# Row maxima of two head groups in five units of score matmuls in place of six

## The chip, the cores and the metric

The kernel runs on one core of a Trainium2 chip. The metric is the device time of one execution in microseconds (us), as the median of several runs. The engines are TensorE (PE in the profile; PEld is its weight load), VectorE (DVE), ScalarE (ACT), GpSimd (POOL) and SyncE (SP, which issues most DMAs). TensorE writes into PSUM, and the other engines read it from there.

## The reference

One decoder layer for B = 4 batches of S = 512 positions and D = 512 features, 16 heads of 32 features, all in fp32. Each of the three parts adds to `x`:

```python
x = x + self_attention(layernorm(x))      # q, k, v and output projections with biases, causal
x = x + cross_attention(layernorm(x), ctx)  # q = layernorm(x), k = v = ctx, causal with a bias of -10000
h = layernorm(x)
shared = relu(h @ W_up.T) @ W_down.T
rw = softmax(top_2(h @ W_gate.T))         # 8 experts
x = x + shared + sum(rw) * (h @ W_expert)
```

Self attention: `softmax(where(causal, q k^T / sqrt(32), -inf)) v`. Cross attention fills masked scores with -10000 in place of -inf.

## The kernel before

All weights stay in SBUF. A head group `g` is four heads: 4 x 32 = 128 features, one chunk of 128 partitions, so there are four groups. The 512 positions make four blocks of 128.

**Two passes over the scores.** The softmax needs each row's maximum before the exponentials. `with_maxima` computes scores with queries on the partitions (tile `sm`) only to get the maxima; `attend` computes them again with keys on the partitions (tile `sc`), subtracts the maximum by a matmul with a bf16 row (`mrow`), and takes the exponential.

**`maxima(g, blocks)`** (L267) does one unit. It takes two PSUM tiles of two banks each (`pair`; two heads per tile, one per bank), and for each block `i` and each head one matmul with 32 contracted rows: 128 queries of block `i` against the (i + 1) x 128 keys up to its end. Causality makes the width 128, 256, 384 or 512. Then for each of the two tiles ScalarE copies it to an SBUF tile `s` (L292), and GpSimd masks the diagonal squares (L298). The reductions on VectorE (L310, result `nm`) come back as a list of jobs. After block 3 of a group `split(g)` (L323) puts the maxima into bf16 parts in `parts[g % 2]`; `rows(g)` (L334) transposes these on TensorE (tile `mt`) and copies the result to `mrow` (L344).

**`with_maxima(steps, a, first, norms)`** (L780) goes through the units of the four groups: blocks (0, 1), block 2 and block 3 of each, twelve in all, with 384, 384 and 512 columns. Between the units it puts matmuls of other work (the fill) in portions by `cost`: query, key and value projections of this or the next batch, or the FFN of the batch before. While a unit's fill runs, the jobs of the unit before are handed to VectorE, one per fill matmul. `rows(g - 1)` goes into the fill of unit (g, 3), so three of the four transposes stand in the fill; the function returns group 3, which `attend` does at n = 4. `norms` are the layernorm jobs of the next batch, added to every other unit. In fill steps named `share` and `gate` a whole step counts as one; all others count as four matmuls.

**`attend(a, late)`** (L810) runs the units (0), (1), (2, 3) of key blocks of each group: scores and exponentials (L360 to L404), and two units later the product with the values (`values`, tile `pv`).

**What sets the order.** TensorE, VectorE, ScalarE and GpSimd take their instructions in the order in which the program writes them (`manual_schedule` with `BY_HAND`); only SyncE's DMAs are ordered by the framework. Semaphores are placed by the framework: a tile that reuses a buffer waits for the readers of the tile before it. PSUM has four pairs (`ps`, bufs=4), which `sm`, `sc`, `pv`, `mt` and the fill's accumulators share. The SBUF tiles `s` use the tags `pt0`, `pt1`, `pt2` (two buffers each) that the exponentials of `attend` use as well.

**The eight stages.** Each batch has one `with_maxima` for self attention and one for cross attention. Their fill has 36, 34, 34 and 16 steps (self, batches 0 to 3) and 20, 36, 20 and 25 steps (cross). Before a cross stage `norm_cross(e, made, t)` transposes the normalised rows in two halves, and ScalarE copies each half into `cqT` (L257), which holds the queries of that stage; one fill step (four matmuls) stands between the two calls for the halves, none after the second. In batch 0's self stage the first `skip` = 3 steps run before the units. The FFN's `gate` (L717) takes the top experts: four maxima and a chain of small operations on VectorE with one exponential on ScalarE within it.

Of the kernel before, what the change touches and what calls it, by code (L numbers as in the profile page):

```python
# [9 lines left out]
F32 = mybir.dt.float32  # L10
# [8 lines left out]
P = 128  # L19
# [7 lines left out]
def decoder_layer(  # L27
# [111 lines left out]
    for r in range(HG):  # L139
# [14 lines left out]
        pattern=[[-1, S]],  # L154
# [13 lines left out]
        pattern=[[-P, NT], [0, HG]],  # L168
# [91 lines left out]
    class Attention:  # L260
# [3 lines left out]
            self.more, self.sums, self.rden, self.e = {}, {}, {}, None  # L264
            self.added = () if cross else range(NC - 1)

        def maxima(self, g, blocks):  # L267

            if blocks[0] == 0:
                self.nm[g] = small.tile([P, NT, HG], F32, tag="nm", name=f"nm_{self.name}_{g}")
            first = blocks[0]
            scs = [pair(f"sm_{self.name}_{g}_{first}_{n}") for n in range(2)]
            at = {i: sum((k + 1) * P for k in blocks if k < i) for i in blocks}
            N = sum((i + 1) * P for i in blocks)
            for i in blocks:
                for r in range(HG):
                    h = slice(r * HD, (r + 1) * HD)
                    nc.tensor.matmul(  # L280
                        scs[r // 2][:, r % 2, at[i] : at[i] + (i + 1) * P],
                        lhsT=self.q_t[h, g, i * P : (i + 1) * P],
                        rhs=self.k_t[h, g, : (i + 1) * P],
                        start=(i == first),
                        stop=True,
                        skip_group_check=(i != first),
                    )
            made = []
            for n in range(2):
                W, tag = {0: (S, "pt0"), 2: (N, "pt1"), 3: (S, "pt2")}[first]  # L290
                s = work.tile([P, 2, W], F32, tag=tag, name=f"s_{self.name}_{g}_{first}_{n}")
                nc.scalar.copy(s[:, :, :N], scs[n][:, :, :N])  # L292
                if len(blocks) > 1:

                    diagonal = s.rearrange("p u (k q) -> p (u k) q", k=2)[:, :, :P]
                else:
                    diagonal = s[:, :, N - P : N]
                nc.gpsimd.affine_select(  # L298
                    out=diagonal,
                    in_=diagonal,  # L300
                    compare_op=ALU.is_ge,
                    fill=NEG,
                    base=0,
                    pattern=[[0, 2 * len(blocks)], [-1, P]],
                    channel_multiplier=1,
                )
                made.append(s)

            def largest(n, i):
                nc.vector.tensor_reduce(  # L310
                    self.nm[g][:, i, 2 * n : 2 * n + 2],
                    made[n][:, :, at[i] : at[i] + (i + 1) * P],
                    axis=AX.X,
                    op=ALU.max,
                    negate=True,
                )

            jobs = [(lambda n=n, i=i: largest(n, i)) for n in range(2) for i in blocks]
            if blocks[-1] == NT - 1:
                jobs.append(lambda: self.split(g))  # L320
            return jobs

        def split(self, g):  # L323
# [445 lines left out]
    def run(steps):  # L769
        for step in steps:  # L770
            for _ in step() or ():
                pass
# [7 lines left out]
    def with_maxima(steps, a, first=0, norms=()):  # L780


        norms = list(norms)
        run(steps[:first])
        fill = matmuls(steps[first:])
        total = sum(1 if step.__name__ in ("share", "gate") else NC for step in steps[first:])
        units = [(g, i) for g in range(NC) for i in ((0, 1), (2,), (3,))]
        cost = [sum(k + 1.5 for k in i) for _, i in units]
        done, due, jobs = 0, 0.0, []
        for n, (g, i) in enumerate(units):  # L790
            new = a.maxima(g, i)
# [12 lines left out]
            jobs = new  # L804
        for _ in fill:
            pass
        run(jobs)
        return NC - 1

    def attend(a, late):  # L810

        units = [(g, j) for g in range(NC) for j in ((0,), (1,), (2, 3))]
        waiting = []

        def values():
            g, j, pts = waiting.pop(0)
            a.values(g, j, pts)
            if g in a.added and j != (2, 3):
                a.add_up(*waiting[0])

        for n, (g, j) in enumerate(units):
            waiting.append((g, j, a.scores(g, j)))
            if n == 4:
                for copy in a.rows(late):
                    copy(nc.scalar.copy)
            if len(waiting) > 2:
                values()
            if a.cross and j == (0,):
                behind(a.e, g)
            if a.cross and j == (2, 3):  # L830
                a.masked(g)
        while waiting:
            values()

    with tc.manual_schedule(engines=BY_HAND):
        e, norms, turns = norm_in(0, x0)
# [3 lines left out]
        nc.gpsimd.tensor_scalar(bqs_sb, bq_sb, SCALE, None, ALU.mult)  # L840
        add_bias(e)
        between_self = query_key(e) + value(e)
        skip, between_cross, ahead = 3, [], []
        for b in range(B):
            more = b + 1 < B
            sa = Attention(e.q_t, e.k_t, e.v, False, f"s{b}")
            norms, turns = [], []
            if more:
                after, norms, turns = norm_in(b + 1)
            late = with_maxima(between_self, sa, skip, norms)  # L850
# [5 lines left out]
            made = out_projection(e, sa, context(e) + turns)  # L856
# [7 lines left out]
            late = with_maxima(steps[3:], ca)  # L864
# [7 lines left out]
            made = add_cross(e, ca)  # L872
# [20 lines left out]
            skip = 0  # L893
# [50 lines left out]
```

## Time and profile before

| | |
|---|---|
| median of three runs | 825.18 us (825.09 to 825.27) |
| the profiled execution | 825.04 us, span 823.3 us |
| busy: PE, DVE, ACT, POOL | 813.3, 544.6, 398.0, 298.3 us |
| reductions L310 | 256, 193.0 us |
| copies L292 of `sm`: 768 wide, 1024 wide | 128 of 0.80 us, 64 of 1.02 us |
| masks L298 | 192, 93.1 us |

The span is the time from the first to the last instruction. Busy time of an engine is the union of its instructions. Matmuls overlap each other in the trace, since the next one starts to stream before the last has drained; the distance between starts is what a matmul costs. A wait that is named after "<-" tells which engine's instruction ended the idle time. The timeline's lines give the start, the length, the engine, the line of the code, the operation, the tiles written and read, and the count.

### The profile page before, as it was taken

The page shows a single profiled execution, that of the slowest core. Times are in us where ns is not written, and L with a number is a line of the kernel's source. Part 1 is how long each engine was busy: PE and PEld are TensorE (multiplying, and loading weights), DVE is VectorE, ACT ScalarE, POOL GpSimd, SP SyncE. Part 2 cuts the span into 40 slices and gives each one's busy share as a digit, 9 for nine tenths or more (in the row PEclk, how much of TensorE's full clock was granted, in tenths as well). Part 3 has the DMA queues.
Part 4 walks back from the last instruction along what each step waited for, and adds up shares of the span by engine and source line. Part 5 has one row for each costly group of instructions (what it writes and reads, how often), then busy time and mean ns, then how long its engine had stood idle before and what let it go on. Part 6 is the DMA issues. An engine that isn't in the chain of part 4 may idle for free.

```text
span 823.3 us, 14456 instructions
## 1 busy us (share of the span) xinstructions
PE 813.3 (99%) x5800; PEld 368.8 (45%) x5800; DVE 544.6 (66%) x937; ACT 398.0 (48%) x502; POOL 298.3 (36%) x549
## 2 busy tenths in 40 slices
PE   8999999999999999999999999999999999999998
PEld 7344454444444454334534445444543444444543
DVE  2578735967678834587868873596779835887512
ACT  2456526762456515556155652676257814565110
POOL 4434512343334732224233471244234643343100
PEclk9999999999999999999999999999999999999999
DMA  9600000001010000030100000000102000000101
GB/s 340 236 27 15 1 1 1 2 2 52 1 39 14 2 1 1 0 103 2 52 14 14 1 2 0 1 2 2 53 3 74 29 1 0 1 2 2 52 0 51
DMA packets 13539, 24.54 MB, mean 30 GB/s; under 512 B 1952, under 2 KB 1952, under 8 KB 13472
## 3 DMA queue, kind: packets, MB, share of 16 engines
q1 hardware_dynamic: 13184, 23.09, 8.3%
q8 instruction: 45, 0.74, 0.4%
q10 hardware_dynamic: 288, 0.52, 0.2%
q14 instruction: 22, 0.18, 0.1%
HBM read 19.42 MB, written 4.19 MB: 29 GB/s over the span
## 4 chain that ended last, share of the span: by engine, by line
PE 94%; DVE 3%; ACT 1%; issue 1%; DMA 0%; POOL 0%; ACTq 0%
PE pm_qk L233 13%; PE pv_c L429 9%; PE pm_d L221 7%; PE pm_u L233 7%; PE pm_v L221 7%; PE pm_o L638 7%; PE pm_e L221 6%; PE pv_s L429 6%; PE sm_c L280 6%; PE sc_s L370 6%; PE sc_c L370 5%; PE sm_s L280 5%; DVE nm_s L310 1%; PE sc_s L381 1%; PE sc_c L381 1%; PE tp_x L666 1%
## 5 line engine op out<-in xcount | busy, mean ns | idle before, releaser
L310 DVE TENSOR_REDUCE nm_c<-s_c 128x2 f32<-128x256 f32 (+3 forms) x128 | 96.3, 810 | 36.6 <-POOL s_c L298 36.6
L310 DVE TENSOR_REDUCE nm_s<-s_s 128x2 f32<-128x256 f32 (+3 forms) x128 | 96.7, 810 | 24.4 <-POOL s_s L298 24.4
L292 ACT COPY s_s<-sm_s 128x768 f32<-128x768 f32 (+1 forms) x96 | 78.8, 874 | 69.0 <-PE sm_s L280 51.2
L292 ACT COPY s_c<-sm_c 128x768 f32<-128x768 f32 (+1 forms) x96 | 78.9, 875 | 48.7 <-PE sm_c L280 34.1
L402 ACT ACTIVATE pt_c<-sc_c 128x768 f32<-128x768 f32 (+1 forms) x96 | 78.5, 884 | 29.3 <-PE sc_c L381 24.8
L298 POOL TENSOR_SCALAR_AFFINE_SELECT s_c<-s_c 128x256 f32<-128x256 f32 (+1 forms) x96 | 46.5, 485 | 118.5 <-ACT s_c L292 117.4
L404 POOL TENSOR_SCALAR_AFFINE_SELECT pt_c<-pt_c 128x256 f32<-128x256 f32 (+1 forms) x96 | 57.4, 605 | 70.5 <-ACT pt_c L402 69.5
L298 POOL TENSOR_SCALAR_AFFINE_SELECT s_s<-s_s 128x256 f32<-128x256 f32 (+1 forms) x96 | 46.6, 488 | 91.4 <-ACT s_s L292 90.6
L458 DVE TENSOR_TENSOR sum_s<-sum_s,pt_s 128x512 f32<-128x512 f32 (+1 forms) x72 | 63.1, 914 | 7.6 <-PE pv_s L429 6.6
L221 PE MATMUL pm_d<-wdown_sb,hT 128*128 128x512 f32 x128 | 61.7, 611 | 0.0
L221 PE MATMUL pm_e<-wexp_sb,fT 128*128 128x512 f32 x128 | 61.2, 608 | 0.4 <-DVE x L760 0.4
L233 PE MATMUL pm_u<-fT,wup_sb 128*128 128x512 f32 x128 | 60.6, 609 | 0.0
L402 ACT ACTIVATE pt_s<-sc_s 128x768 f32<-128x768 f32 (+1 forms) x72 | 55.8, 837 | 9.4 <-PE sc_s L381 7.0
L370 PE MATMUL sc_s<-qT,kT 32*128 32x128 f32 (+3 forms) x512 | 57.4, 466 | 1.9 <-DVE x L760 1.3
L233 PE MATMUL pm_qk<-xnT,wk_sb 128*128 128x512 f32 x120 | 59.3, 612 | 0.0
L221 PE MATMUL pm_v<-wv_sb,xnT 128*128 128x512 f32 x128 | 58.8, 600 | 0.0
L638 PE MATMUL pm_o<-wo_sb,oT_s 128*128 128x512 f32 x128 | 57.8, 596 | 0.0
L233 PE MATMUL pm_qk<-xnT,wq_sb 128*128 128x512 f32 x120 | 57.6, 606 | 0.0
L404 POOL TENSOR_SCALAR_AFFINE_SELECT pt_s<-pt_s 128x256 f32<-128x256 f32 (+1 forms) x72 | 48.4, 676 | 21.4 <-ACT pt_s L402 20.0
L370 PE MATMUL sc_c<-cqT,ckT 32*128 32x128 f32 (+3 forms) x512 | 51.5, 467 | 1.3 <-ACT pt_c L402 1.3
L280 PE MATMUL sm_c<-ckT,cqT 32*128 32x512 f32 (+3 forms) x512 | 49.4, 468 | 0.0
L280 PE MATMUL sm_s<-kT,qT 32*128 32x512 f32 (+3 forms) x512 | 48.1, 467 | 0.0
(148 smaller groups left out, 1183.5 us busy)
## 6 DMA issues: line engine op xcount, KB each, us to landing
cv<-in_ctx_dram SPq DMA_DIRECT2D x16, 256.0 KB, 4.2
out_dram<-x SPq DMA_DIRECT2D x16, 256.0 KB, 2.0
x<-in_x_dram SPq DMA_DIRECT2D x14, 256.0 KB, 4.1
xin<-in_x_dram SPq DMA_DIRECT2D x12, 256.0 KB, 2.6
wq_sb<-in_wq_dram SPq DMA_DIRECT2D x2, 512.0 KB, 6.0
wk_sb<-in_wk_dram SPq DMA_DIRECT2D x2, 512.0 KB, 7.7
wv_sb<-in_wv_dram SPq DMA_DIRECT2D x1, 1024.0 KB, 8.3
wo_sb<-in_wo_dram SPq DMA_DIRECT2D x1, 1024.0 KB, 9.9
```

Source lines behind the costliest of these rows:

```text
L221: nc.tensor.matmul(pm, lhsT=lhs_t[:, c, t * P : (t + 1) * P], rhs=w[:, c, :], start=(c == 0), stop=(c == NC - 1),)
L233: nc.tensor.matmul(pm, lhsT=w[:, c, f * P : (f + 1) * P], rhs=rhs_t[:, c, :], start=(c == 0), stop=(c == NC - 1),)
L280: nc.tensor.matmul(scs[r // 2][:, r % 2, at[i] : at[i] + (i + 1) * P], lhsT=self.q_t[h, g, i * P : (i + 1) * P], rhs=self.k_t[h, g, : (i + ...
L292: nc.scalar.copy(s[:, :, :N], scs[n][:, :, :N])
L298: nc.gpsimd.affine_select(out=diagonal, in_=diagonal, compare_op=ALU.is_ge, fill=NEG, base=0, pattern=[[0, 2 * len(blocks)], [-1, P]], cha ...
L310: nc.vector.tensor_reduce(self.nm[g][:, i, 2 * n : 2 * n + 2], made[n][:, :, at[i] : at[i] + (i + 1) * P], axis=AX.X, op=ALU.max, negate=True,
L370: nc.tensor.matmul(scs[r // 2][:, r % 2, at[j] : at[j] + S - j * P], lhsT=self.k_t[h, g, j * P : (j + 1) * P], rhs=self.q_t[h, g, j * P :] ...
L402: nc.scalar.activation(pt[:, :, :N], scs[n][:, :, :N], AF.Exp)
L404: nc.gpsimd.affine_select(out=diagonal, in_=diagonal, compare_op=ALU.is_ge, fill=0.0, base=0, pattern=[[0, 2 * len(blocks)], [1, P]], chan ...
L429: nc.tensor.matmul(pv[r * HD : (r + 1) * HD, u, j * P :], lhsT=ones if u else self.v[:, j, h * HD : (h + 1) * HD], rhs=pts[r // 2][:, r % ...
L458: nc.vector.tensor_tensor(to, to, pts[n][:, :, at[j] : at[j] + S - j * P], ALU.add)
L638: nc.tensor.matmul(pms[t // 2][:, t % 2, :], lhsT=a.out[:, c, t * P : (t + 1) * P], rhs=wo_sb[:, c, :], start=(c == 0), stop=(c == NC - 1),)
```

## The change

`maxima` takes a list of pieces (group, block) in place of a group and its blocks. Two groups are now done in five units: blocks 2 and 0 of the one, blocks 2 and 0 of the other, block 1 of both, block 3 of the one, block 3 of the other. Each unit fills 512 columns of every bank. The tiles `s` are 512 wide and take the tags `pt0` and `pt2` in turn; `pt1` is no longer used here. The fill is shared equally between the ten units. `rows(0)` and `rows(1)` stand in units 5 and 6 (counted from 0); `rows(2)` is done in `attend` at n = 1 and `rows(3)` at n = 4, both with the copy on ScalarE. A norm is added to every unit until there are none left. In batch 0's self stage four steps run ahead instead of three.

```diff
-        def maxima(self, g, blocks):
+        def maxima(self, pieces, tag):
...
-            at = {i: sum((k + 1) * P for k in blocks if k < i) for i in blocks}
-            N = sum((i + 1) * P for i in blocks)
-            for i in blocks:
+            at, N = [], 0
+            for g, i in pieces:
+                at.append(N)
+                N += (i + 1) * P
...
+            for (g, i), c in zip(pieces, at):
                 for r in range(HG):
                     h = slice(r * HD, (r + 1) * HD)
                     nc.tensor.matmul(
-                        scs[r // 2][:, r % 2, at[i] : at[i] + (i + 1) * P],
+                        scs[r // 2][:, r % 2, c : c + (i + 1) * P],
                         lhsT=self.q_t[h, g, i * P : (i + 1) * P],
                         rhs=self.k_t[h, g, : (i + 1) * P],
...
-                W, tag = {0: (S, "pt0"), 2: (N, "pt1"), 3: (S, "pt2")}[first]
-                s = work.tile([P, 2, W], F32, tag=tag, name=f"s_{self.name}_{g}_{first}_{n}")
-                nc.scalar.copy(s[:, :, :N], scs[n][:, :, :N])
+                s = work.tile([P, 2, S], F32, tag=tag, name=f"s_{name}_{n}")
+                nc.scalar.copy(s, scs[n])
...
-        units = [(g, i) for g in range(NC) for i in ((0, 1), (2,), (3,))]
-        cost = [sum(k + 1.5 for k in i) for _, i in units]
+        units = []
+        for g in range(0, NC, 2):
+            units += [[(g, 2), (g, 0)], [(g + 1, 2), (g + 1, 0)], [(g, 1), (g + 1, 1)]]
+            units += [[(g, NT - 1)], [(g + 1, NT - 1)]]
         done, due, jobs = 0, 0.0, []
-        for n, (g, i) in enumerate(units):
-            new = a.maxima(g, i)
-            if norms and n % 2 == 0:
+        for n, pieces in enumerate(units):
+            new = a.maxima(pieces, f"pt{n % 2 * 2}")
+            if norms:
                 new.append(norms.pop(0))
-            due += total * cost[n] / sum(cost)
-            for k in range(round(due) - done):
+            due += total / len(units)
+            count = round(due) - done
+            for k in range(count):
                 next(fill, None)
                 done += 1
-                if k == 1 and i[-1] == NT - 1 and g > 0:
-                    jobs = a.rows(g - 1) + jobs
+                if k == min(1, count - 1) and n in (5, 6):
+                    jobs = a.rows(n - 5) + jobs
                 run(jobs[:1])
                 jobs = jobs[1:]
             run(jobs)
             jobs = new
         for _ in fill:
             pass
+        late = {1: 2, 4: NC - 1}
+        if total > 40:
+            run(a.rows(late.pop(1)))
         run(jobs)
-        return NC - 1
+        return late
...
-            if n == 4:
-                for copy in a.rows(late):
+            if n in late:
+                for copy in a.rows(late[n]):
                     copy(nc.scalar.copy)
...
-        skip, between_cross, ahead = 3, [], []
+        skip, between_cross, ahead = 4, [], []
```

More of the change, by code (lines that the diff above doesn't have):

```diff
@@ L265, in __init__ @@
             self.added = () if cross else range(NC - 1)
-        def maxima(self, g, blocks):
[L271 to L274, printed above, removed]
-            at = {i: sum((k + 1) * P for k in blocks if k < i) for i in blocks}
-            N = sum((i + 1) * P for i in blocks)
-            for i in blocks:
+        def maxima(self, pieces, tag):
[3 more added lines that the diff above has]
+                N += (i + 1) * P
+                if g not in self.nm:
+                    self.nm[g] = small.tile(
+                        [P, NT, HG], F32, tag="nm", name=f"nm_{self.name}_{g}"
+                    )
+            name = f"{self.name}_{pieces[0][0]}_{pieces[0][1]}"
+            scs = [pair(f"sm_{name}_{n}") for n in range(2)]
+            for (g, i), c in zip(pieces, at):
                 for r in range(HG):
@@ L280, in maxima @@
                     nc.tensor.matmul(
-                        scs[r // 2][:, r % 2, at[i] : at[i] + (i + 1) * P],
+                        scs[r // 2][:, r % 2, c : c + (i + 1) * P],
                         lhsT=self.q_t[h, g, i * P : (i + 1) * P],
                         rhs=self.k_t[h, g, : (i + 1) * P],
-                        start=(i == first),
+                        start=(c == 0),
                         stop=True,
-                        skip_group_check=(i != first),
+                        skip_group_check=(c > 0),
                     )
@@ L289, in maxima @@
             for n in range(2):
-                W, tag = {0: (S, "pt0"), 2: (N, "pt1"), 3: (S, "pt2")}[first]
-                s = work.tile([P, 2, W], F32, tag=tag, name=f"s_{self.name}_{g}_{first}_{n}")
-                nc.scalar.copy(s[:, :, :N], scs[n][:, :, :N])
-                if len(blocks) > 1:
-                    diagonal = s.rearrange("p u (k q) -> p (u k) q", k=2)[:, :, :P]
+                s = work.tile([P, 2, S], F32, tag=tag, name=f"s_{name}_{n}")
+                nc.scalar.copy(s, scs[n])
+                if len(pieces) == 1:
+                    diagonal = s[:, :, S - P :].unsqueeze(2)
+                elif pieces[0][1] == pieces[1][1]:
+                    diagonal = s.rearrange("p u (k q) -> p u k q", k=2)[:, :, :, P:]
                 else:
-                    diagonal = s[:, :, N - P : N]
+                    diagonal = s[:, :, S - 2 * P :].rearrange("p u (k q) -> p u k q", k=2)
                 nc.gpsimd.affine_select(
@@ L303, in maxima @@
                     base=0,
-                    pattern=[[0, 2 * len(blocks)], [-1, P]],
+                    pattern=[[0, 2], [0, len(pieces)], [-1, P]],
                     channel_multiplier=1,
@@ L307, in maxima, with largest @@
                 made.append(s)
-            def largest(n, i):
+            def largest(n, g, i, c):
                 nc.vector.tensor_reduce(
                     self.nm[g][:, i, 2 * n : 2 * n + 2],
-                    made[n][:, :, at[i] : at[i] + (i + 1) * P],
+                    made[n][:, :, c : c + (i + 1) * P],
                     axis=AX.X,
@@ L316, in largest @@
                 )
-            jobs = [(lambda n=n, i=i: largest(n, i)) for n in range(2) for i in blocks]
-            if blocks[-1] == NT - 1:
-                jobs.append(lambda: self.split(g))
+            jobs = [
+                (lambda n=n, g=g, i=i, c=c: largest(n, g, i, c))
+                for n in range(2)
+                for (g, i), c in zip(pieces, at)
+            ]
+            if pieces == [(pieces[0][0], NT - 1)]:
+                jobs.append(lambda: self.split(pieces[0][0]))
             return jobs
```

## The prediction

> **What bounds the kernel now.** I read the page first, then busy time by stage, then the timeline of one stage. Names: S0 to S3 and C0 to C3 are the eight stages of `with_maxima` (self, cross; batch 0 to 3).
>
> ```profile
> span 823.3 us, 14456 instructions
> PE 813.3 (99%) x5800; PEld 368.8 (45%) x5800; DVE 544.6 (66%) x937; ACT 398.0 (48%) x502; POOL 298.3 (36%) x549
> PEclk9999999999999999999999999999999999999999
> PE 94%; DVE 3%; ACT 1%; issue 1%; DMA 0%; POOL 0%; ACTq 0%
> ```
>
> TensorE is busy for 99% at full clock, so only two things count: TensorE time that the edit removes, and waits that it puts in front of TensorE. The profiled execution took 825.04 us (1.74 outside the span); the median of three runs is 825.18. Now C0 and S3 by stage (window, length, PE, PEld, DVE, ACT, POOL busy, clock):
>
> ```profile
> 127.50:159.30 31.80, 31.80 (x182) 12.57 (x180) 24.85 (x46) 22.91 (x30) 11.26 (x24) 1.00 0.00 1
> 602.00:630.40 28.40, 27.99 (x174) 10.62 (x173) 24.57 (x44) 20.73 (x26) 11.21 (x24) 1.00 0.05 19
> ```
>
> VectorE is the second engine; in S3 it is busy from 604.56 to 638.1, so it nearly binds there. The timeline of C0's start:
>
> ```profile
> 126.58 1.04 PE L249 MATMUL tp_q<-ident,xn_q 128*128 128x128 f32 x8
> 127.54 0.94 PE L280 MATMUL sm_c<-ckT,cqT 32*128 32x128 f32 x16
> 127.65 1.02 ACT L257 ACTIVATE cqT<-tp_q 128x1024 f32<-128x1024 f32 x1 [3.00 <-PE tp_q L249]
> 128.41 1.98 PE L233 MATMUL pm_qk<-xnT,wk_sb 128*128 128x512 f32 x4
> 130.33 0.93 PE L280 MATMUL sm_c<-ckT,cqT 32*128 32x384 f32 x8
> 131.18 1.12 PE L233 MATMUL pm_qk<-xnT,wk_sb 128*128 128x512 f32 x2
> 132.24 1.14 PE L280 MATMUL sm_c<-ckT,cqT 32*128 32x512 f32 x8
> 133.31 1.13 PE L233 MATMUL pm_qk<-xnT,wk_sb 128*128 128x512 f32 x2
> ```
>
> Read the starts, not the durations, which overlap. A matmul is two passes, and in a long run a 512-column pass takes 0.43 (118.83 to 122.27 holds eight). Fill stretches cost 0.20 more than their passes (128.41 to 130.33: 1.92 for four). So do units: 0.87 for blocks 0 and 1 and 0.85 for block 2 against 0.64 of streaming, 1.07 for block 3 against 0.86. That is the price of switching between 128-row and 32-row tiles.
>
> **The change, part by part.** The built order shows ten units in place of twelve per stage, the same matmuls, reductions and bytes. No stage has over 40 steps, so the new `total > 40` branch never runs.
>
> 1. *Fewer switches.* A pair of groups had 2 x (0.87 + 0.85 + 1.07) = 5.58. Now three two-piece units of 512 columns cost 0.86 + 0.23 = 1.09 at most and two cost 1.07: about 5.39. That is 0.20, and with one fill stretch less (0.20) it is 0.40 a pair; 16 pairs give **-6.4**. Bounds: 0.35 to 0.45, so -5.6 to -7.2.
>
> 2. *`rows(2)` leaves the fill.* Its transposes cost 2.14 - 1.92 = 0.22 at C0's end (157.19 to 159.33) and 0.28 inside a stretch (S0). Eight stages: **-2.0**. They return inside the wait of part 3.
>
> 3. *`rows(2)` enters the attention at n = 1.* Here are the exponentials of the attention's start and what they release:
>
> ```profile
> 160.76 4.75 ACT L402 ACTIVATE pt_c<-sc_c 128x1024 f32<-128x1024 f32 x6 [0.28 <-issue]
> 161.84 0.70 PE L370 MATMUL sc_c<-cqT,ckT 32*128 32x256 f32 x4 [0.23 <-ACT pt_c L402]
> 162.75 0.31 PEld L370 LDWEIGHTS sc_c<-cqT,ckT 32*128 32x128 f32 x8 [0.62 <-ACT pt_c L402]
> 163.77 1.06 PE L429 MATMUL pv_c<-pt_c,cv 128*32 128x512 f32 x8
> ```
>
> TensorE runs into the four PSUM pairs: the scores of blocks 2 and 3 wait for the first and the second exponential, and the first values start 1.02 after the second wait ends. In the built order the new transpose tile takes the first pair. So those scores wait for the second and third exponentials. Behind them stand the values, on which everything else of the attention depends. The third exponential ends 0.70 after the second (768-wide ones start 0.70 apart: four in 2.93), so the first values start 0.70 later. The copy of the row is now ScalarE's at 0.59 instead of VectorE's 0.42; it stands behind the fourth exponential and ends at about +5.2 us, before the first values do (+6.1 in self, +7.0 in cross), so it costs nothing more; uncovered it would be 0.59. Eight stages at 0.70: **+5.6** (0 if TensorE waited there anyway, 10.3 with the copy uncovered; the exponential rows are the nearest, so 0.70).
> The Trainium skill, Perfetto Trace Analysis, Optimizing Scalar/DVE Operations, puts the access overhead on PSUM at about 51 ns for Scalar and 125 for DVE. By that alone the moved copy would be 0.07 us shorter on ScalarE, while these rows have it 0.17 longer, and the rows decide.
>
> 4. *Block 2 comes first.* In the cross stages the first unit was blocks 0 and 1, which need only the first half of `cqT`. Block 2 needs the half that ScalarE is still copying: 127.65 to 128.67, while the old unit ran at 127.54. The built order has this wait on the first score matmul, with all fill queued behind it on TensorE. Start at 128.73: 1.2 each in C0, C1 and C2; in C3 the copy ends at 688.73 instead of a start at 687.56 that already lost 0.36, so 0.9. **+4.5** (bounds 3.9 to 4.8; no other work stands before it). Self stages take Q and K by group; `skip = 4` keeps group 1 in time.
>
> 5. *The gate.* Its max, exponential and sums stand on VectorE ahead of the reductions of the unit before. Before, in S1:
>
> ```profile
> 235.46 0.39 DVE L729 MAX8 top<-lg 128x8 f32<-128x8 f32 x4 [0.24 <-PE lg L720]
> 236.32 0.16 DVE L736 TENSOR_REDUCE es<-ew 128x4 f32<-128x8 f32 x1 [0.27 <-ACT ew L734]
> 237.27 2.33 DVE L310 TENSOR_REDUCE nm_s<-s_s 128x2 f32<-128x1024 f32 x2
> ```
>
> Now it falls in unit 5 of S1 and S2, with `rows(1)` already due in unit 6 rather than four units after. Counted from unit 5's start: the gate's exponential waits behind two copies of 1024 (to 1.23 + 1.93 = 3.16); VectorE is free at 4.35; one reduction 1.17, the row copy 0.35, the other 1.17 and `split` 0.95 end at 8.0. TensorE reaches `rows(1)` at 1.08 + 0.91 + 1.03 + 0.22 + 1.01, then 1.08 + 1.82: 7.15. Wait 0.9, twice. In C3 the gate falls in unit 3 and holds up unit 2's reductions, for which ScalarE's copies wait as only two sets of score buffers are left; unit 5 then waits about 0.7 for PSUM and `rows(0)` about 0.5 for `split`. **+3.0** (0 to 5).
>
> 6. *Small ones.* In S1 and S2 a unit now needs the pair that ReLU frees, behind copies of 1.93 instead of 1.50: **+0.3**. In C0, C2 and C3 units that waited (135.22: 1.08 for 0.87; 148.03: 1.26 for 1.07) no longer meet that neighbour: **-1.0**. S3: VectorE has 33.1 us (33.5 less the 0.42 copy) from about +2.9, so the last reduction of group 2, for which the second exponential's buffer waits, ends only at about +30.5 of the stage; 1.02 for that exponential, 0.75 to the end of the next and 1.02 of scores put the first values at +33.3, where they were (635.28 - 601.96), and the stage's gain is lost: **+0.5**. ScalarE has 32 copies less (2 x 1.02 for 2 x 0.80), PoolE 32 masks less, both under slack; norms of the next batch move up to units 0 to 4, under TensorE's 4 us a unit.
> Against larger copies, the Trainium skill's same page and section says that breaking up instructions can finish work sooner where Scalar or Vector are not saturated but cause bubbles elsewhere. In these rows only the ReLU place of part 6 is of that kind. If it held at every unit, at 0.43 each, 80 units would add 34 us; C0 leaves ScalarE idle for over a quarter.
>
> Sum: -6.4 - 2.0 + 5.6 + 4.5 + 3.0 + 0.3 - 1.0 + 0.5 = **+4.5**, so 829.5 by the profiled execution and about 829.6 by the median. About 0.2% (1.65 us) can be told from no change.
>
> **Rivals.** *The gate is harmless*: VectorE has caught up before it, and parts 5 and S3 fall away: +1.0, 826.1, no change. For it: VectorE is idle for a quarter of S1. Against: idle time in front of the gate cannot be used by reductions queued behind it. *Faster*: the attention is paced by ScalarE from its start, so that the late first values cost nothing and the waits at the next scores (about 0.2 in four stages) go as well. Then part 3 is 0, the sum is -1.1 - 0.8, and the time 823.1; this decides if ScalarE never waits for TensorE in the attention. Against: the page has `pt_c` idle 29.3, of which 24.8 is released by TensorE. *VectorE binds*: two sets of score buffers instead of three couple ScalarE to VectorE in all short stages. 25.5 of reductions, 4.6 of `split`, 0.8 of rows make 30.9 in C0 against 30.6 of TensorE. If that costs 1.5 in C0 and C2 and 2 in S3, it is +9.5: 834.5. Against: the last reductions may end in the attention.
>
> **How the numbers follow.** My forecast 0.56 (826.9 to 832.5, from parts 1, 3 and 5); gate harmless 0.20 (824.9 to 827.3); faster 0.06; VectorE binds 0.18. Slower: 0.56, 0.18 and a quarter of the second, 0.79. Same: 0.15 of the second; faster: 0.06. The range leaves out the faster case and the upper half of the last: 824.8 to 834.0.
>
> **What would show it.** Right: the first `sm_c` of C0 to C2 waits 1.2 for ACT cqT; the first `pv` comes 5.1 after the first `sc`, not 4.4; `mt` waits 0.9 for DVE in S1 and S2; a fill stretch and unit still lose 0.4 together. Wrong: no wait at `cqT`, or a ramp of 4.4.

## The result, and the profile after

The changed kernel takes 832.82 us (median of four runs, 832.60 to 834.66) against 825.14 in the same comparison: ratio 1.0098, 95% interval 1.0085 to 1.011. It is slower by 7.7 us; 4.5 were forecast. The profiled execution took 832.77 us, so the two traces differ by 7.5 in the span, and that is the difference explained below. Single executions of most of these kernels stand in two groups some 1.5 us apart (those of the kernel before do not; the last section has the reason), so medians are given, with the profiled execution beside them where it is of the other group.

The page's lines of after, and the windows of C0 and S3 from their first score matmul to the first of the attention (window, length, PE, PEld, DVE, ACT, POOL busy, granted clock; then the share and GB/s of the DMAs):

```profile
span 830.8 us, 14315 instructions
PE 810.7 (98%) x5800; PEld 377.8 (45%) x5800; DVE 539.0 (65%) x929; ACT 400.7 (48%) x478; POOL 288.6 (35%) x517
PEclk9999999999999999999999999999999999999999
PE 90%; DVE 6%; ACT 2%; issue 1%; DMA 0%; POOL 0%
```
```profile
128.42:159.14 30.72, 30.50 (x176) 12.89 (x176) 24.54 (x42) 21.55 (x24) 10.63 (x19) 1.00 0.00 1
605.20:634.85 29.65, 27.69 (x170) 11.75 (x169) 23.76 (x41) 20.40 (x22) 10.62 (x19) 1.00 0.05 18
```

TensorE's busy time went down by 2.6 us (813.3 before) and the span went up by 7.5, so the time in which TensorE does nothing grew by 10.1: the loss is all waits. The chain moved from PE to DVE, 3% to 6%. C0's stage itself is shorter by 1.07, S3's is longer by 1.21 and has 1.96 us in which TensorE does nothing. What TensorE waits for, by the view of waits (total, times, longest):

```profile
PE sm_c L284 <- ACT cqT L257: 4.5, 4, 1.2
PE mt_s L347 <- DVE parts L341: 4.5, 5, 1.3
PE sc_c L379 <- ACT pt_c L411: 2.0, 4, 0.5
PE sc_s L379 <- ACT sum_s L411: 1.6, 3, 0.5
PE mt_c L347 <- DVE parts L341: 1.6, 3, 1.2
```

The first line is new, and it is part 4; `mt` waiting for VectorE's `parts` is new too, five times in self (once in S1, once in S2, three times in S3) and three times in cross (once in C0, C2 and C3). The timeline of C0's start and of its attention's start:

```profile
127.34 1.02 ACT L257 ACTIVATE cqT<-tp_q 128x1024 f32<-128x1024 f32 x1 [3.00 <-PE tp_q L249]
128.42 1.15 PE L284 MATMUL sm_c<-ckT,cqT 32*128 32x384 f32 x16 [1.11 <-ACT cqT L257]
129.50 1.98 PE L233 MATMUL pm_qk<-xnT,wk_sb 128*128 128x512 f32 x4
...
160.53 3.34 ACT L411 ACTIVATE pt_c<-sc_c 128x1024 f32<-128x1024 f32 x4
161.60 0.38 PE L347 MATMUL mt_c<-identb,parts 128*128 128x128 bf16 x4
162.52 1.40 PE L379 MATMUL sc_c<-cqT,ckT 32*128 32x256 f32 x12 [0.53 <-ACT pt_c L411]
163.73 0.62 ACT L353 COPY mrow_c<-mt_c 128x512 bf16<-128x512 bf16 x1
164.24 1.06 PE L438 MATMUL pv_c<-pt_c,cv 128*32 128x512 f32 x8
```

A unit and its fill still lose 0.4 together: 128.42 to 129.50 is 1.08, and the next unit starts at 131.41, 1.91 for four matmuls. The first values start 5.10 after the first scores (159.14) in place of 4.44.

By stage, each from the first values of the stage before to its own first values (S0 from the span's start), against what the parts of the prediction add up to:

| | parts of the prediction | measured |
|---|---|---|
| S0 | -0.35 | -0.31 |
| C0, C1, C2 | +0.45, +0.85, +0.45 | +0.78, +0.72, +0.77 |
| S1, S2 | +0.7, +0.7 | +0.67, +0.60 |
| S3 | +0.15 | +1.86 |
| C3 | +1.55 | +2.40 |

Six stages are right within 0.35. The last batch carries 2.56 of the 3.0 that are missing.

### The profile page after: what moved, and what is told of

Same layout as the page of the kernel before. It is cut to its first block, busy times and chain, and to the rows that moved or that the text cites. A ratio compares the mean times of both kernels' runs of the same rounds, so it can differ in the third digit from the quotient of the medians.

```text
span 830.8 us, 14315 instructions
## 1 busy us (share of the span) xinstructions
PE 810.7 (98%) x5800; PEld 377.8 (45%) x5800; DVE 539.0 (65%) x929; ACT 400.7 (48%) x478; POOL 288.6 (35%) x517
## 4 chain that ended last, share of the span: by engine, by line
PE 90%; DVE 6%; ACT 2%; issue 1%; DMA 0%; POOL 0%
PE pm_qk L233 13%; PE pv_c L438 9%; PE pm_u L233 7%; PE pm_v L221 7%; PE pm_o L647 7%; PE pm_e L221 6%; PE pv_s L438 6%; PE sc_s L379 6%; PE pm_d L221 6%; PE sc_c L379 5%; PE sm_c L284 5%; PE sm_s L284 4%; DVE nm_s L315 2%; PE sc_s L390 1%; PE sc_c L390 1%
## 5 line engine op out<-in xcount | busy, mean ns | idle before, releaser
L315 DVE TENSOR_REDUCE nm_c<-s_c 128x2 f32<-128x768 f32 (+3 forms) x128 | 96.1, 810 | 42.8 <-POOL s_c L303 42.8
L315 DVE TENSOR_REDUCE nm_s<-s_s 128x2 f32<-128x768 f32 (+3 forms) x128 | 96.3, 809 | 28.7 <-POOL s_s L303 28.6
L295 ACT COPY s_s<-sm_s 128x1024 f32<-128x1024 f32 x80 | 77.8, 1015 | 67.5 <-PE sm_s L284 45.4
L295 ACT COPY s_c<-sm_c 128x1024 f32<-128x1024 f32 x80 | 77.5, 1015 | 51.5 <-PE sm_c L284 36.9
L303 POOL TENSOR_SCALAR_AFFINE_SELECT s_c<-s_c 128x512 f32<-128x512 f32 (+1 forms) x80 | 44.2, 553 | 122.4 <-ACT s_c L295 122.4
L303 POOL TENSOR_SCALAR_AFFINE_SELECT s_s<-s_s 128x512 f32<-128x512 f32 (+1 forms) x80 | 44.5, 556 | 117.1 <-ACT s_s L295 117.1
L413 POOL TENSOR_SCALAR_AFFINE_SELECT pt_c<-pt_c 128x256 f32<-128x256 f32 (+1 forms) x96 | 55.3, 582 | 75.7 <-ACT pt_c L411 74.8
L233 PE MATMUL pm_qk<-xnT,wk_sb 128*128 128x512 f32 x120 | 57.3, 607 | 0.0
L284 PE MATMUL sm_c<-ckT,cqT 32*128 32x512 f32 (+3 forms) x512 | 46.7, 460 | 4.5 <-ACT cqT L257 4.5
```

What stands on the lines that cost most here:

```text
L233: nc.tensor.matmul(pm, lhsT=w[:, c, f * P : (f + 1) * P], rhs=rhs_t[:, c, :], start=(c == 0), stop=(c == NC - 1),)
L284: nc.tensor.matmul(scs[r // 2][:, r % 2, c : c + (i + 1) * P], lhsT=self.q_t[h, g, i * P : (i + 1) * P], rhs=self.k_t[h, g, : (i + 1) * P] ...
L295: nc.scalar.copy(s, scs[n])
L303: nc.gpsimd.affine_select(out=diagonal, in_=diagonal, compare_op=ALU.is_ge, fill=NEG, base=0, pattern=[[0, 2], [0, len(pieces)], [-1, P]], ...
L315: nc.vector.tensor_reduce(self.nm[g][:, i, 2 * n : 2 * n + 2], made[n][:, :, c : c + (i + 1) * P], axis=AX.X, op=ALU.max, negate=True,)
L413: nc.gpsimd.affine_select(out=diagonal, in_=diagonal, compare_op=ALU.is_ge, fill=0.0, base=0, pattern=[[0, 2 * len(blocks)], [1, P]], chan ...
```

## Experiments

The theory: part 3 is the third exponential's PSUM pair, part 4 the second half of `cqT`, and the rest TensorE waiting for `split`, which in the last batch is VectorE's amount of work. The rival is that VectorE and ScalarE are bound together by two sets of `s` and that any wait taken away comes back. The time of after is 832.8 throughout.

**Block 1 first in the cross stages.**

```diff
+            three = [[(g, 2), (g, 0)], [(g + 1, 2), (g + 1, 0)], [(g, 1), (g + 1, 1)]]
+            if a.cross and g == 0:
+                three = three[2:] + three[:2]
```

> The changed kernel, except that in the cross stages the shared unit with block 1 of groups 0 and 1 goes first, ahead of the two units with blocks 2 and 0. Block 1 needs only the first half of cqT. My theory (part 4): the first score matmul no longer stands behind ScalarE's copy of the second half; C0, C1 and C2 get 1.19 us back each, C3 about 0.85 (1.15 less the 0.3 that it also lost before): -4.4, so 828.4 us by the median of 832.8. The rival: ScalarE still has that copy ahead of its first two copies of scores (1.93 us), so that the next units wait for PSUM and over half is given back: 830.5 or more.

Measured: 828.17 us, ratio to before 1.004 (1.0027 to 1.0052), so -4.65. C0, C1 and C2 start 1.19, 1.17 and 1.18 earlier, and the line of `sm_c <- ACT cqT` is gone from the waits. Their stages and starts are otherwise the same to 0.01, so nothing is given back there. In the profiled execution (829.51) the clock is at half for 3.41 us behind S3's last wait, S3's first values come 0.57 later, and C3 starts only 0.22 earlier. C3's share is thus not read from the trace; the median has it. Part 4 stands with its size.

**The two late rows at n = 4 and 7.**

```diff
-        late = {1: 2, 4: NC - 1}
+        late = {4: 2, 7: NC - 1}
...
-            run(a.rows(late.pop(1)))
+            run(a.rows(late.pop(4)))
```

The last two lines stand in the branch that never runs.

> The changed kernel, except that rows(2) and rows(3) are done in the attention at n = 4 and n = 7 in place of n = 1 and n = 4: the same work, away from the start. My theory (part 3): the scores of blocks 2 and 3 wait again for the first two exponentials, the first values start 4.40 us after the first scores in place of 5.09, and 0.65 to 0.70 comes back in each of eight stages; S3 may keep some of it, since VectorE is late there: -5.0 to -5.4, so about 827.6 us. The rival: the tile mt takes a PSUM pair from whatever comes next, wherever it stands, and the attention loses the same 0.65 at n = 7: 832.5.

Measured: 831.55 us, ratio 1.0078 (1.0066 to 1.0091): only -1.3. All eight starts came back to 4.39, 6.04 in all, and the attentions gave back 0.70 in S0, S1 and S2 each, 1.29 in S3, 0.33 in C0, C1 and C3 each and 0.55 in C2. The mistake was mine: I had priced `rows` away from the start at the pair alone. The timeline of a self attention at n = 7:

```profile
272.15 0.40 PE L347 MATMUL mt_s<-identb,parts 128*128 128x128 bf16 x4
272.48 0.86 PE L438 MATMUL pv_s<-pt_s,v 128*32 128x256 f32 x16
273.27 1.12 PE L379 MATMUL sc_s<-qT,kT 32*128 32x256 f32 x12
274.02 0.33 PE L390 MATMUL sc_s<-mrow_s,onesb 32*128 32x256 bf16 x4
```

The transposes take 0.33 of TensorE (272.15 to 272.48), and the scores of blocks 2 and 3 take 1.43 (273.27 to the next values at 274.70) where a group without `mt` takes 1.07. So 0.70 is what `rows` costs at n = 7 of a self attention (at n = 4 the changed kernel's trace has the same 0.33 and 1.44), and at the start the transposes are free but the pair is not.

**Rows 0 and 1 later.**

```diff
-                if k == min(1, count - 1) and n in (5, 6):
-                    jobs = a.rows(n - 5) + jobs
+                if k == min(1, count - 1) and n in (6, 8):
+                    jobs = a.rows(n // 2 - 3) + jobs
```

> The changed kernel, except that rows(0) and rows(1) are due in units 6 and 8 in place of 5 and 6. The waits of mt for VectorE's split in the changed kernel, from the distances between starts: 0.83 in S1 and S2 each, 0.38 in C0, C1 and C2 each, 0.74 and 1.36 in S3, 1.32 in C3, 6.2 in all. My theory: TensorE comes too early to a split that would be done a unit later, so all but S3's go (there VectorE is behind to the end and the start of the attention waits in their place): -4.1, so 828.7 us. The rival, VectorE binds: the time comes back in front of rows(2) and the exponentials in every stage with the gate, -1 at most, 831.8 or more.

Measured: 832.75 us, ratio 1.0088 (1.0074 to 1.0101): nothing. Both theories are half right. S1 and S2 gain 0.84 and 0.85, C0 and C2 0.37 and 0.39, of which their starts give back 0.12 each, as expected of a split that is done a little later. (C1, for which the expectation also lists 0.38, has no such wait in the changed kernel.) S3 and C3 lose 2.16: S3's stage 0.21, its first values 0.47, its attention 0.87, C3's stage 0.61, there with a score unit that waits 2.26 for an addition on VectorE (L759). The two parts in the middle, 1.34, are not all a wait: from 637.29 this execution has 3.41 us at half clock, which the changed kernel's profiled one does not have. The one execution of the four with a granted clock of 0.999 (the others have 0.997 or 0.998) took 831.03, 1.8 less than the changed kernel's median. So in the last batch the wait for VectorE came back elsewhere, with 0.82 more in the two stages; in the other batches it went.

**Three tags for `s`, two rotations.** First `f"pt{n % 3}"`, then `f"pt{(n + 2) % 3}"`.

> The changed kernel, except that the tiles s take the tags pt0, pt1 and pt2 in turn, so that ScalarE can be three units ahead of VectorE's reductions in place of two. My theory: only the waits of score units for PSUM that come from copies held back by reductions go (0.40 and 0.28 in C3, about 0.15 three times in S3, 0.3 in S1): -0.9, so 831.9 us. The rival of the prediction, VectorE binds through two sets: it was priced at 5.0 over C0, C2 and S3, so 828 us; S3 alone would give back 1.5 or more.

Measured: 848.93 us, ratio 1.0291 (1.0277 to 1.0305). Neither: slower by 16. The last unit (n = 9) now holds `pt0`, which the first exponentials of a cross attention need, and these wait for its reductions. The lines are C0's, whose first values come 1.64 later; the eight starts lose 9.0, and three stretches at half clock, 13.7 us together, add to it:

```profile
162.22 3.55 ACT L411 ACTIVATE pt_c<-sc_c 128x1024 f32<-128x1024 f32 x4 [1.44 <-DVE nm_c L315]
163.29 0.38 PE L347 MATMUL mt_c<-identb,parts 128*128 128x128 bf16 x4 [1.39 <-DVE nm_c L315]
```

So this run tells nothing about the number of sets, but that the tag of the last unit matters. With the other rotation:

> The changed kernel with three tags for s, but rotated so that the last three units hold pt0, pt1 and pt2 in this order, the order in which the exponentials take them; with the rotation of the earlier run the first exponentials of the cross attentions waited for the reductions of the last unit (1.44 us of ScalarE's idle time in C0, first values 1.63 later). My theory: what is left of that run's loss goes, and against two sets only the short waits of score units for PSUM and a part of S3's late start are saved: -1.2, about 831.6 us. The rival (two sets bind VectorE to ScalarE): 5 us back, 827.8.

Measured: 836.14 us, ratio 1.0138 (1.0123 to 1.0153). The cross starts are 5.14 again, and it is still slower than with two tags, by 3.3. The stages of C0 and C2, where the rival had put 1.5 each, are the same to 0.01: two sets do not bind there, and that rival of the prediction is out for them. The loss lies in S1 and S2 (0.52 and 0.51) and in S3 and its attention (2.5). In the stages it is the same wait, for `split`, made longer; in S3's attention 3.41 us at half clock (from 641.18) are a part of it, so S3 alone does not settle the rival. VectorE and GpSimd in S1:

```profile
240.05 0.49 DVE L337 CAST parts<-nm_s 128x16 bf16<-128x16 f32 x1
240.76 0.64 POOL L303 TENSOR_SCALAR_AFFINE_SELECT s_s<-s_s 128x512 f32<-128x512 f32 x1 [0.28 <-ACT s_s L295]
240.79 0.66 DVE L340 CAST parts<-rest_s 128x16 bf16<-128x16 f32 x1
241.49 0.23 DVE L341 TENSOR_TENSOR parts<-rest_s,parts 128x16 bf16<-128x16 f32 x1
```

A cast of 16 elements takes 0.20 elsewhere; here it takes 0.66 and ends 0.05 after the mask that was running. With a third set ScalarE copies the second tile without waiting (with two it waits 0.34 for a reduction there), so the mask starts at 240.76 and falls on the split; with two sets it starts at 241.29, when the split is done.

**The row copy of `rows(2)` on VectorE.**

```diff
-                    copy(nc.scalar.copy)
+                    copy(nc.vector.tensor_copy if n == 1 else nc.scalar.copy)
```

> The changed kernel, except that the copy of mrow after rows(2) at n = 1 is VectorE's in place of ScalarE's. It asks what the 0.70 us at the attention's start is made of. Theory A, the PSUM pair that the tile mt takes: the first values still come 5.09 us after the first scores, and the time stays within 0.8 of 832.8; VectorE does the copy after its last reductions, at about +4.7 to +5.0, and holds the pair a little longer. Theory B, ScalarE's 0.59 us stands between the exponentials that are waited for: the first values come at 4.5, -4.7 in all, 828.1 us.

Measured: 855.85 us, ratio 1.0371 (1.0356 to 1.0387), slower by 23. Theory B is out: the start is later without the copy on ScalarE, 5.96 in self and 6.83 in cross (8.45 and 7.52 in the last batch). But "within 0.8" is out too. The values' tile now takes the pair that `mt` held, and VectorE frees it last, behind its reductions and, in cross, behind a scan. In self the view names the copy as what ended the wait (0.79, DVE mrow_s). In cross, below, it names a mask that ends a little after the copy, but in all eight starts the values begin 0.14 to 0.15 after the end of the copy:

```profile
165.01 1.21 DVE L632 TENSOR_TENSOR_SCAN behT<-ckT,zero 128x511 f32<-128x511 f32 x1
166.14 0.39 DVE L353 COPY mrow_c<-mt_c 128x512 bf16<-128x512 bf16 x1
166.68 1.94 PE L438 MATMUL pv_c<-pt_c,cv 128*32 128x512 f32 x8 [1.66 <-POOL pt_c L413]
```

The eight starts lose 13.1 in all. The attentions of C0, C1, S3 and C3 lose another 2.8, 2.6, 2.0 and 1.7, and there the clock was at half, as told at the end; C2's, with the same waits at full clock, loses nothing.

**Transposes into spare columns.** The scores of key block 1 fill 384 of the 512 columns of a bank; the four transposes fit into the rest of one tile.

```diff
...
+                spare = scs[0][:, :, N:].bitcast(BF16)
+                copies = self.rows(extra, [spare[:, i // 2, i % 2 * P : (i % 2 + 1) * P] for i in range(NT)], spare)
...
-            waiting.append((g, j, a.scores(g, j)))
-            if n in late:
-                for copy in a.rows(late[n]):
-                    copy(nc.scalar.copy)
+            waiting.append((g, j, a.scores(g, j, late.get(n))))
```

> The changed kernel, except that the transposes of rows(2) and rows(3) at n = 1 and n = 4 write into the 128 columns of a bank that the scores of key block 1 leave free, so that mt takes no PSUM pair of its own; same instructions otherwise. Theory A (the pair costs the 0.70 us): at n = 1 the transposes (0.33) hide in the wait for the first exponential, the first values come at 4.40, -5.2 to -5.6 over eight stages with S3's part uncertain; at n = 4 the 0.37 of self attention that goes beyond the transposes' own 0.33 goes too, -1.5: 825.9 us. Theory B (ScalarE's copy, or the transposes' own time): at most 0.4 a stage, 829.6 or more.

Measured: 835.09 us, ratio 1.0123 (1.0107 to 1.0138), slower by 2.3 (1.8 by the profiled execution, 834.61). Seven starts gained only 0.27, and S3's lost 0.69. My reading is that the copy of the row keeps the first tile's pair, so the values take the pair of the fourth exponential, and at n = 4 both exponentials stand behind the transposes (0.46 lost in each self attention, 0.22 to 0.57 in cross). It says which tile to take, the second (`scs[1]`):

> As the run with the spare columns, but the transposes go into the free columns of the second score tile of key block 1 in place of the first. In that run the copy of the row kept the pair that the third exponential would have freed, so the first values took the pair of the fourth (they came at 4.83 in place of 5.09), and at n = 4 both exponentials stood behind the transposes (0.46 lost in each self attention, 0.25 in each cross). Now the pair of the third exponential is free and the first exponential of the unit doesn't stand behind them. Theory A (the number of pairs that stand between the scores and the first values sets the 0.70): first values at 4.40, -5.2 to -5.6, and at n = 4 no more than 0.2 lost: about 827.5 us. Theory B (the transposes and the copy cost what they cost wherever they stand): as that run, 833 or more.

Measured: 829.27 us, ratio 1.0044 (1.0032 to 1.0057), -3.5 by the median and -4.9 by the profiled execution (827.89, at full clock like the changed kernel's). The start of C0:

```profile
159.85 3.35 ACT L417 ACTIVATE pt_c<-sc_c 128x1024 f32<-128x1024 f32 x4
160.90 0.40 PE L349 MATMUL sc_c<-identb,parts 128*128 128x128 bf16 x4
162.86 1.06 PE L446 MATMUL pv_c<-pt_c,cv 128*32 128x512 f32 x8
163.06 0.62 ACT L355 COPY mrow_c<-sc_c 128x512 bf16<-128x512 bf16 x1
```

Same transposes, same copy on the same engine, and the values start 4.39 after the first scores (158.47); seven starts gained 0.70, S3's none. The attentions are the same in S0 to S2, 0.40 shorter in S3 and 0.10 longer in cross. Together with the two runs before it this shows what part 3 only argued: the 0.70 is the pair that the values or the scores of blocks 2 and 3 must wait for, not the copy and not the transposes.

**Half the maxima in the last batch.** In S3 and C3 each reduction reads the first half of its columns only, and the other half is left out.

```diff
-                    made[n][:, :, c : c + (i + 1) * P],
+                    made[n][:, :, c : c + (i + 1) * P // (2 if self.name[1] == "3" else 1)],
```

> The changed kernel, except that in the last batch's two stages (S3, C3) each maximum is taken over the first half of the columns only, which leaves out half of VectorE's 25 us of reductions there and nothing else. It measures how much of S3 and C3 VectorE's work costs. My theory: the waits of mt for split in S3 (0.74 and 1.36) and C3 (1.32), of the score units for PSUM in C3 (0.9 in all), and 0.44 of S3's late first values go: -4.5, so 828.3 us. The rival, the order of the queue: VectorE stands idle in S3 for 1.39 us before an addition that waits for TensorE's pm_e, with reductions queued behind it, and its shorter work shortens no wait that this sets: half of it stays, 830.5 or more.

Measured: 829.63 us, ratio 1.0055 (1.0038 to 1.0072): -3.2 of the 4.5. VectorE's busy time in S3's stage went from 23.76 to 15.96 us. C3 gains 1.77, and its waits in front of `rows(0)` (1.32) and of unit 5 (0.40) are gone. S3 gains 0.92 in the stage and 0.43 at the start. Of its two waits for `split` (0.74 and 1.36 by the distances between starts; the lines below give the idle time alone, 0.07 less) the second is gone and 0.54 of the first stays; there the queue's order sets it. S3 of the changed kernel, VectorE and then the three transposes of TensorE that wait for it:

```profile
616.23 1.22 DVE L315 TENSOR_REDUCE nm_s<-s_s 128x2 f32<-128x1024 f32 x1 [0.21 <-POOL s_s L303]
618.84 1.41 DVE L769 SCALAR_TENSOR_TENSOR x<-pm_e,rw,x 128x512 f32<-128x512 f32 x2 [1.39 <-PE pm_e L221]
620.16 1.21 DVE L315 TENSOR_REDUCE nm_s<-s_s 128x2 f32<-128x1024 f32 x1
622.17 0.23 DVE L341 TENSOR_TENSOR parts<-rest_s,parts 128x16 bf16<-128x16 f32 x1
625.99 0.23 DVE L341 TENSOR_TENSOR parts<-rest_s,parts 128x16 bf16<-128x16 f32 x1
638.73 0.23 DVE L341 TENSOR_TENSOR parts<-rest_s,parts 128x16 bf16<-128x16 f32 x1
622.46 0.40 PE L347 MATMUL mt_s<-identb,parts 128*128 128x128 bf16 x4 [0.67 <-DVE parts L341]
626.28 0.40 PE L347 MATMUL mt_s<-identb,parts 128*128 128x128 bf16 x4 [1.29 <-DVE parts L341]
639.02 0.40 PE L347 MATMUL mt_s<-identb,parts 128*128 128x128 bf16 x4 [1.19 <-DVE parts L341]
```

The first line is one of the two reductions that `split(0)` needs, the third is the other. Between them the experts' addition stands idle for 1.39 until TensorE has done its `pm_e`, and then takes 1.41. From 618.84 on VectorE has a line behind it: `split(2)` ends at 638.96, 4.1 after the attention began at 634.85, and `rows(2)` waits for it.

**Parts put together.** Block 1 first, the second tile's spare columns, and rows 0 and 1 in units 6 and 8 except in the last batch:

```diff
-                if k == min(1, count - 1) and n in (5, 6):
-                    jobs = a.rows(n - 5) + jobs
+                when = (5, 6) if a.name[1] == "3" else (6, 8)
+                if k == min(1, count - 1) and n in when:
+                    jobs = a.rows(when.index(n)) + jobs
```

> The changed kernel with three parts of the runs put together: block 1 first in the cross stages (-4.65), the transposes of rows(2) and rows(3) in the second tile's spare columns (-5.3 forecast), and rows(0) and rows(1) in units 6 and 8 in all stages but those of the last batch, where that cost more than it gave (-0.85 in S1 and S2 each, -0.25 in C0 and C2 each: -2.2). If they act on different waits, 832.8 - 12.1 = 820.7 us, under the kernel before (825.1). If rows later only move the wait to the start of the attention, 823.

Measured: 820.95 us, ratio to before 0.9956 (0.9943 to 0.9968), where 820.7 was expected (the profiled execution, 822.42, has one stretch at half clock). By what the runs measured, 4.65, 4.9 and 2.2, the sum is 11.75, and it came to 11.9: the parts act on different waits and add up. And with the last batch's row copies of groups 0 and 1 on ScalarE:

```diff
+                    if when[0] == 5:
+                        jobs.pop(0)(nc.scalar.copy)
```

> The same three parts, and in the last batch's stages ScalarE does the row copies of rows(0) and rows(1), which takes 4 x 0.42 us from VectorE there. If VectorE's amount of work sets the end of S3 and C3, each gains up to 0.8: 819.5 us. If the order in its queue sets it, or ScalarE's copy of scores stands behind a copy that waits for split, it is the same or slower: 820.7 or more.

Measured: 820.07 us, ratio 0.9943 (0.993 to 0.9957), the fastest: 5.0 under before and 12.7 under after. The step from the run before it (0.9) is near the width of the intervals. What TensorE still waits for after the program's first 20 us:

```profile
PE mt_s L349 <- DVE parts L341: 1.7, 2, 1.1
PE sc_s L349 <- DVE parts L341: 1.3, 1, 1.3
PE mt_c L349 <- DVE parts L341: 1.2, 1, 1.2
```

All four waits are in the last batch, for VectorE. Last, the kernel before with the spare columns only:

> The kernel before (six units for two groups, its own fill and queue order), with one thing changed: rows(2) leaves the fill for n = 1 of the attention, rows(3) stays at n = 4, and both transpose into the spare columns of the second score tile of key block 1, with the copy on ScalarE. It takes part 2 of the prediction (-2.0: 0.22 to 0.28 in each of eight stages) by itself, without the packing of units and without the pair that part 3 lost. My theory: -2.0 and no change of the start (4.40): 823.1 us, so that the five units with all that was mended (820.1) are still worth 3. The rival: the kernel before had no wait at the start for this to hide in, and the transposes' 0.33 comes back there or at n = 4: 825 us.

Measured: 823.70 us, ratio 0.9981 (0.9972 to 0.999), -1.6. The eight stages are shorter by 0.22 to 0.28 each, 1.96 in all, which is part 2; 0.10 is given back in each of four cross attentions. The starts stay at 4.40 in self and 4.44 in cross but for S3's, which is 0.32 later. So the five units with all their mending are ahead of the six with the spare columns by 0.38 points of ratio, some 3 us. Whether the six would gain as well from the last batch's row copies on ScalarE no run shows.

## Why the prediction was right, and where it fell short

*The number.* 832.8 is inside the range, but 0.3 above the band given to the case that was held likely (826.9 to 832.5). The range holds it because it took in the lower half of "VectorE binds", and what carried the time there is VectorE in the last batch, not the coupling in C0 and C2 that was priced under that name. That much of it is luck.

*What bounds.* Right: TensorE's clock stayed full in the changed kernel's profiled execution and its waits grew by more than the whole loss.

*Parts 1 and 2.* Right. (The working's 5.39 is 5.41 by its own terms; with the measured 1.08 and 1.07 it is 5.38.) C1 meets no new wait within its stage and became 1.11 shorter: 0.28 is `rows(2)`, and 0.83 are two pairs at 0.40. The spare-column run of the kernel before has part 2 by itself at -1.96 against -2.0.

*Part 3.* Right in cause and size: 0.65 to 0.70 in each of eight stages, 5.4 against 5.6. That the copy on ScalarE costs nothing also held, since the values take another pair than the one it holds. What the prediction did not see is that the transposes' place has a second price. Where they stand in a wait they are free; at n = 7 of a self attention they cost the same 0.70, and at n = 7 of a cross attention 0.33 in three of four.

*Part 4.* Right: 4.65 by the run that takes it away, 4.5 forecast; 3.54 of it is read in the trace, in C0 to C2.

*Part 5.* Right for S1 and S2 (0.83 of waiting against 0.9). C3 was sized at 1.2 and is 2.0: 1.32 in front of `rows(0)`, 0.40 and 0.28 in two units for PSUM. The mechanism, VectorE kept from its reductions by the gate and catching up too late, is the one named; half the maxima removes all but the 0.28. The gate's first instruction in C3 shows it, with unit 2's reductions queued behind it although their masks were done at 704.67:

```profile
706.83 0.39 DVE L738 MAX8 top<-lg 128x8 f32<-128x8 f32 x4 [4.59 <-PE lg L729]
```

*Part 6.* This is the step that failed, and it holds most of the missing 3 us. The term "+0.5" for S3 assumed that VectorE works without a pause from +2.9 on, and that only the attention's start meets its end. Instead VectorE stood idle for 1.39 in front of the experts' addition, and TensorE came to `rows(0)` and `rows(1)` before their `split`, 0.74 and 1.36, waits that the working did not list at all. The path at the start was another, too: the working let an exponential wait for a buffer that the last reduction of group 2 frees at +30.5. No exponential of S3's start waits for a reduction. The transposes of `rows(2)` wait 1.19 for `split(2)`, which ends 33.8 after the stage's first scores, and the first values come 1.36 behind those transposes, at +35.2 instead of +33.3. These waits make S3 +1.86 where +0.15 came out of the parts. The working counted when VectorE's last job ends and never checked the three `split` jobs that TensorE waits for. The vanished waits of C0 and C2 did vanish, but each got a new one of 0.38 at `rows(1)`. The timeline shows what made it:

```profile
148.84 0.64 POOL L303 TENSOR_SCALAR_AFFINE_SELECT s_c<-s_c 128x512 f32<-128x512 f32 x1 [1.66 <-ACT s_c L295]
148.94 0.60 DVE L340 CAST parts<-rest_c 128x16 bf16<-128x16 f32 x1
149.86 0.40 PE L347 MATMUL mt_c<-identb,parts 128*128 128x128 bf16 x4 [0.22 <-DVE parts L341]
```

TensorE was there at 149.48 (147.66 and 1.82 for four matmuls). The cast is 0.40 longer than its usual 0.20, and the wait is that 0.40.

*The rivals.* "Gate harmless" and "faster" are out by the waits in S1 and the later starts. "VectorE binds" was right about S3 and wrong about C0 and C2, whose stages a third set of buffers leaves as they are. In S3 less work on VectorE made it better, and a third set did not help.

## What to carry to other kernels

Packing the same matmuls into fewer, fuller units saves its switches as counted (0.83 for two pairs of groups in C1, 0.80 forecast); whether it pays is decided by what the new order puts beside a wait, here the operand half that comes last, the PSUM pair at a ramp, and a transpose one unit after the work that feeds it. List for each stage every job that the bounding engine waits for, not only the last one, and ask at each when its engine gets to it in queue order, with the instruction that stands in front of it. A tile that needs a buffer of its own for a moment may fit into columns that a neighbour leaves free; take the neighbour that is freed last anyway.

## What the runs showed of the hardware

**A busy GpSimd stretches some VectorE instructions.** GpSimd's masks read and write the SBUF copies; in no row of the changed kernel's trace does GpSimd read PSUM. In the changed kernel and the run with three sets, a bf16 cast or a two-input operation of 16 elements took 0.26 to 0.69 in place of 0.18 to 0.23 when it met a mask, and ended within 0.1 of the mask's end. The reductions did not stretch: in the changed kernel the 1024-wide ones took 1.21 with a mask running for over 0.2 of it (38 of them) and without (26). The Trainium skill, SBUF — State Buffer, Who interferes with whom, says that a VectorE instruction in a two-port mode and GpSimd shut each other out for a whole instruction, that one with two SBUF inputs contends with a GpSimd instruction that reads SBUF, and that one with at most one SBUF input outside those modes does not contend. These rows agree, if the casts ran in a two-port mode, which no run here shows.

**A short thinning of TensorE's work can halve its clock.** In the run with the copy on VectorE, windows of C0's attention start (length, busy PE, PEld, DVE, ACT, POOL, granted clock):

```profile
162.30:164.10 1.80, 1.26 (x14) 0.69 (x16) 1.73 (x4) 1.80 (x3) 1.02 (x4) 1.00 0.00 0
164.10:166.70 2.60, 0.94 (x24) 0.70 (x25) 2.33 (x6) 1.99 (x3) 1.51 (x4) 0.84 0.00 0
166.70:168.40 1.70, 1.70 (x11) 0.44 (x14) 0.00 (x0) 0.00 (x0) 0.54 (x1) 0.50 0.00 0
171.50:172.50 1.00, 1.00 (x8) 0.17 (x4) 0.78 (x2) 0.08 (x1) 0.00 (x0) 0.50 0.00 0
172.50:174.00 1.50, 1.50 (x23) 0.42 (x16) 1.50 (x2) 0.84 (x1) 0.00 (x0) 0.94 0.00 0
```

TensorE was busy for half of the 4.4 us from 162.30, with two pauses of 0.53 and 1.66, and then ran at half clock from 166.70 to past 172: sixteen 512-column passes of values took 3.57 where they take 1.85 in the changed kernel. In C0 and C1 a wait of 1.7 us thus cost over 4. It does not always happen: C2 has the same pauses (0.53 and 1.67), kept a clock of 1.00 and lost only the wait itself.

The changed kernel's waits, at most 1.3 each, did not do this in its profiled execution, but in others such waits do, and that is why single executions stand in two groups. In the profiled one of the run with block 1 first, S3's last wait is the same 1.19 (until 635.31), and the granted clock is 0.50 from 636.01 to 639.42. The four profiled executions with a mean granted clock of 0.998 (block 1 first, rows 0 and 1 later, three sets in step, parts put together) each have one such stretch of 3.41 us at the start of S3's attention; half of it, 1.7, is near the 1.5 between the groups. The profiled executions of the changed kernel, of the two runs with spare columns in it and of the run with row copies on ScalarE have none. The Trainium skill, TensorE: Matmul & The Clock Gate, What's actually happening, gives half rate after an idle window of about 3.4 us; no pause here was that long, so the rows show the clock halving after less than a fully idle window.
